# A fused state-space and expert layer on one Trainium2 core: low part of the activations by TensorE and ScalarE, stacked router logits, shorter routing, rstd by exp and ln with a Newton step, new due times

## The chip, the core and the metric

The kernel runs on one core of a Trainium2 chip. The core has TensorE (PE; its weight loads are listed apart as PEld), VectorE (DVE), ScalarE (ACT), GpSimd (POOL) and SyncE (SP), which here only issues DMAs. Each engine works through its own queue in order; they meet through semaphores. The metric is the device time of one execution in microseconds, the median of several runs. The profile is one further execution, taken with the hardware profiler.

## The reference

The input `u` has 8 batches of 1024 rows with 256 channels. A small vector `c` per batch gives six modulation vectors. Then, per batch:

```python
h = layernorm(x) * (1 + ca) + sa
x = x + ga * ssm(h)        # selective scan, 16 states per channel
h = layernorm(x) * (1 + cb) + sb
x = x + gb * moe(h)        # 8 experts of 256x256, the best 2 of each row
```

The scan part projects `h` to a step width `dt` (softplus) and to 16 rows each of B and C, runs `h_n[t] = exp(dt*A_n) * h_n[t-1] + dt*u*B_n[t]` over the rows for each of the 16 states n, and sums `h_n * C_n` over n. The expert part takes `softmax(h @ Wg)`, picks the two largest values of each row, divides them by their sum, and adds the two experts' outputs with these gates. Because the choice of experts depends on small differences, the matrix products there are made from a high and a low part of each operand (`hi`, `lo`; `wg_hi`, `wg_lo`; `we_hi`, `we_lo`), each rounded to the matmul's faster type, with the product of the two low parts left out.

## The kernel before, in words

The 8 x 1024 rows are cut into 16 stages of 512 rows (`CL`), two per batch. A stage has three parts, and stages overlap: while one is in its scans, the one before is in its experts and the one after in its front.

- `front(s)`: statistics of the rows (`statistics`, L777 and L780 on DVE), the factors (`factors`), normalised rows (`normalize`, L822, ACT), transposes to channels (`to_channels`, L852, PE), modulation out of PSUM (`modulate`, L863, ACT), projections (L915, L946), softplus (L952).
- `state(s, n)` for n = 0 to 15: a broadcast load of a row of B and of C (`bc`, SP), `v = du * B` (L1012, POOL), two decays `a = exp(dt * A)` (L1023, ACT), two scans (L1034, DVE), and the product with C: on DVE (`hcD`, L1044) for 10 of 16 states on average, on POOL (`hs`, L1049) for the others. PE adds these products up in PSUM with transposing matmuls (L1097).
- `back(s)`: residual add (L1133, DVE), statistics and factors of the second layernorm, normalising, transposes, the high and low part, router logits, routing, expert products (`expert_pair`, L1310, PE), weighting by the gates (L1388, ACT), summing (L1398, PE), and a storing DMA that adds (L1463, issued by POOL). The last stage's back is cut in two halves and ends on DVE (L1333).

The factors of a layernorm are made per stage for 8 values at once (4 groups of 128 rows of the second layernorm, and 4 of the first one two stages later). ACT copies variance plus eps (L800) and the negated mean (L802) into a small tile `ln`; POOL raises to the power -1/2 (L810) and multiplies with the negated mean (L814). ACT's normalising waits for that.

The high and low part: for each of the two channel halves j, the transposed rows lie in a PSUM tile `pt`. ACT writes the modulated value to SBUF as `hi`, rounded (L863), writes the modulated value again in place into `pt` (L863), and DVE writes `lo = pt - hi` (L1169). The logits are six matmuls into 8 PSUM rows (L1195): `hi` with `wg_hi`, `hi` with `wg_lo`, `lo` with `wg_hi`, for two halves each. ACT copies them out (L1202), PE transposes them back (L1206), and 16 small DVE instructions, with an exponential on ACT as the third step, make the gates (L1225 to L1240, then L1244).

The buffers are rings: four of `v`, three PSUM banks of `a`, two of `y`, one of `ma`, and two of `psm`, which serve transposes, projections, logits and expert products alike.

The order of instructions on every engine is written by a planner (`Plan.emit`). Each step has a kind, an engine, an assumed cost and a due time: the time of its stage plus an entry of the table `DUE`, one per kind and, where it has five, per phase (first stage, second, middle, last but one, last). The planner simulates the engines with these costs and always takes the ready step that is due first; `PATIENCE` says how long an engine may be kept idle for a more urgent step. The order so found is fixed by dependencies; what it costs on the chip is another matter.

Of the kernel before, what the change touches and what calls it, by code (L numbers as in the profile page):

```python
# [10 lines left out]
F32 = mybir.dt.float32  # L11
# [6 lines left out]
P = 128  # L18
CL = 512
# [11 lines left out]
AHEAD = 1010.84  # L31
PATIENCE = {"ACT": 0.15, "DVE": 0.31, "PE": 0.32, "POOL": 0.26, "SP": 0}
# [5 lines left out]
    "-1/2": -610.4,  # L38
    "load c": -1959.77,
    "load wmod0": -1959.2,  # L40
    "load wmod1": -1903.73,
    "load wmod2": -1904.33,
    "load wmod3": -1902,
    "load W_x": -1905.67,
    "load W_dt": -1902.95,
    "load b_dt": -1896.67,
    "load A": -1896.69,
    "load D": -1905.33,
    "load Wg": 23.65,
    "Wg hi": 25.6,  # L50
    "Wg lo": -1879.07,
    "c^T": 19.14,
    "exp c": 576.64,
    "1 + exp c": -171.26,
    "1 / c": -583.34,
    "silu c": 49.75,
    "mod1": 597.1,
    "mod1 out": 214.25,
    "mod1 + 1": -23.47,
    "mod2": -1859.82,  # L60
    "mod2 out": -158.07,
    "mod3": 229.79,
    "mod3 out": -128.45,
    "mod3 + 1": -812.43,
    "ga0": -205.9,
    "ga1": -118.55,
    "ga2": -138.57,
    "ga3": -194.1,
    "gb0": 46.87,
    "gb1": 211.85,  # L70
    "gb2": -132.77,
    "gb3": -2055.94,
    "ga mod": -1469.96,
    "ga mod D": 75.2,
    "1 / ga": -434.12,
    "gb^T": -1935.95,
    "gb out": -1918.95,
    "gb store": -2004.44,
    "W_x^T": 597.29,
    "W_x out": -3.67,  # L80
    "W_dt^T": -1851.32,
    "W_dt out": -85.73,
    "exp A": -10.89,
    "-A": -388.67,
    "be rows": -3.96,
    "be hi": -24.41,
    "be lo": -124.92,
    "be": 74.87,
    "eps": -5318.24,
    "gates hi": (-1934.68, -2774.13, 20.33, -39.94, 880.55),  # L90
    "gates lo": (-26.36, -2354.31, -688.15, -51.05, -108.76),
    "load be": -1860.49,
    "iw": -610.42,
    "load x": (-1905.45, -1873.57, -1877.87, -1851.67, -345.66),
    "stats1": (224.71, 130.11, 139.36, -25.7, -59.05),
    "aggr1": (213.04, 114.8, -308.72, -24.67, 2.36),
    "before1": (-102.85, 91.85, 2.54, -14.87, -18.75),
    "rstd1": (-1104.41, -1916.02, -121.49, -268.12, -120.91),
    "shift1": (-507.66, -410.48, -1091.47, 527.46, 48.83),
    "norm1": (-144.62, -217.6, 35.93, 471.97, 36.59),  # L100
    "trans1_0": (-1936.2, -1160.43, -2075.71, -328.08, -365),
    "modg_0": (-1701.88, 396.46, -461.17, -6.71, -105.52),
    "modD_0": (-1695.18, -131.34, -462.04, -397.38, -105.23),
    "trans1_1": (-388.21, -18.09, -54.78, -626.82, -11.83),
    "modg_1": (-50.33, -1935.21, -197.83, -9.86, -10.79),
    "modD_1": (-11.21, -1916.99, -81.27, -9.63, -23.55),
    "W_x / ga": (66.75, 401.9, 25.85, -49.61, 434.89),
    "proj": (-596.85, -706.64, -714.41, -84.24, -74.21),
    "rows": (-2173.39, -2045.69, -3586.53, -10.82, -2052.7),
    "spill": (-4069.73, -5330.21, -46.16, -311.17, 432.09),  # L110
    "dt0": (-45.16, -658.43, -1891.19, -1934.24, -76.75),
    "softplus0": (-1126.61, -39.94, -137.57, -2844.14, -16.53),
    "dt1": (-2318.21, -2801.94, -207.93, -1934.26, -398.3),
    "softplus1": (-1126.2, -132.53, -379.84, -2844.16, -28.04),
    "du": (-195.14, -2811.82, -615.21, -365.67, -2224.29),
    "load B, C": (-5316.63, -1003.95, -1855.19, -4111.06, -3714.47),
    "v": (-12.17, -164.66, 175.11, 576.96, 952.78),
    "a0": (-22.27, -4.61, -6.54, -5.76, -3.99),
    "a1": (-22.41, -4.9, -6.15, -6.69, -4.35),
    "scan0": (-141.18, -335.17, -38.46, -51.65, -37.62),  # L120
    "keep0": (-1141.13, -1001.73, -2670.6, -1274.64, -1043.43),
    "C0": (-158.99, -48.75, -78.37, -397.8, -49.3),
    "scan1": (254.21, -7.15, -37.67, -52.31, -38.52),
    "keep1": (-281.8, -71.4, -191.93, -1247.6, -175.93),
    "C1": (-927.57, -102.36, -383.08, -272.81, -85.21),
    "C": (-434.46, -982.76, -611.91, -346.76, -4070.99),
    "y D": (-45.12, -33.67, -1893.89, -3.99, 105.31),
    "y": (-692.43, -142.1, -4.58, -4.37, -52.76),
    "y C": (-691.09, -2044.02, -79.98, -1517.96, -52.81),
    "load We": -1855,  # L130
    "We hi": -9.52,
    "We lo": -13.87,
    "x + y": (-1479.33, -1886.74, -1168.73, -231.3, 149.03),
    "store x": (-922.68, -81.4, -352.75, -1815.49, -3867.78),
    "stats2": (-1494.52, -143.82, -1171.26, -54.3, -45.3),
    "aggr2": (-211.14, -109.77, -383.59, -45.32, -9.65),
    "before2": (-6.93, 939.25, -95.98, -81.58, 4.88),
    "rstd2": (-1311.51, -927.35, -919.37, -30.48, -1009.27),
    "shift2": (-289.83, -684.01, -16.58, -27.32, -1671.91),
    "norm2": (-1.27, -217.09, 3.69, -457.58, 32.8),  # L140
    "trans2_0": (-119.41, -234.62, -25.53, -50.95, -76.58),
    "hi0": (-141.55, -203.81, -1226.77, -71.08, -264.52),
    "mod2_0": (-2325.4, 23.63, -1516.83, 17.71, 8.96),
    "lo0": (-954.37, -2006.41, -590.6, 934.22, -43.41),
    "trans2_1": (-68.72, -46.84, -1.98, -2278.83, -10.41),
    "hi1": (1.23, -85.95, -1275.97, -1245.79, 101.74),
    "mod2_1": (-321.5, -1489.76, -82.34, 2.7, -325.68),
    "lo1": (-1141.17, -296.15, -3856.65, 5.32, -1526.54),
    "logits^T": (-724.23, -896.69, -969.16, -194.29, -2895.23),
    "logits out": (-1885.54, -25.88, 4.38, -1907.25, -252.75),  # L150
    "logits": (-1228.11, -85.65, -1913.27, -106.24, -61.81),
    "route": (-1101.97, -1134.93, -1307.99, -656.85, -170.03),
    "gates": (-23.84, -155.06, -1508.55, -606.87, -165.13),
    "gates^T": (407.78, -236.26, -474.82, -43.28, -53.64),
    "gates out": (-77.16, -201.21, -201.01, -1117.77, 23.17),
    "biases": (-1847.78, -40.94, -21.25, 21.25, 22.67),
    "expert0": (-47.23, -150.46, 2.39, -24.85, 59.33),
    "weigh0": (-1667.95, -187.39, -1697.15, 581.79, -169.94),
    "sum0": (154.3, 300.84, -65.34, 25.8, 428.26),
    "gb": (-58.36, -0.34, -1235.11, 1080.88, -11.47),  # L160
    "turn": (45.89, -1931.1, -368.57, -9.4, 45.02),
    "out": (15.32, -128.7, -182.23, -5.57, 44.86),
# [4 lines left out]
    "load gb": (-157.01, -157.01, -157.01, -157.01, -165.58),  # L167
    "last bias": -13.22,
    "last": 89.02,
    "last expert": -11.99,  # L170
    "last store": -219.81,
}

# [1351 lines left out]
```

## Time and profile before

| | us |
|---|---|
| median of 3 runs | 1079.51 |
| lowest, highest | 1077.4, 1081.53 |
| the profiled execution, its own time | 1078.12 |
| its span, first to last instruction | 1076.2 |

| engine | busy us | share of the span | instructions |
|---|---|---|---|
| DVE | 976.5 | 91% | 1506 |
| PE | 948.7 | 88% | 5525 |
| POOL | 928.3 | 86% | 454 |
| ACT | 840.0 | 78% | 1835 |

The mean granted TensorE clock is 0.948 of full speed. Busy time counts each engine by itself; PE's is modelled in part, because matmuls are pipelined. A line such as "L1169 DVE TENSOR_TENSOR lo<-pt,hi" names the line of the kernel, the engine, the operation, and the tile that is written from the tiles that are read. Idle time of an engine is listed with what ended it; an engine that isn't the bottleneck may be idle at no cost.

### The profile page before, as it was taken

What the parts mean: (1) busy time and instruction counts of PE and PEld (TensorE: products, weight loads), DVE (VectorE), ACT (ScalarE), POOL (GpSimd) and SP (SyncE); (2) the same over time, 40 slices, a digit from 0 to 9 for tenths busy, and PEclk for the clock granted to TensorE, in tenths of its full rate; (3) what the DMA queues carried; (4) which work ended last, traced back from release to release, by engine and by line L of the source; (5) the groups of instructions that cost most, each with busy time, mean ns of one, the idle gap of its engine ahead of it and who ended that gap; (6) DMA issues with size and microseconds to landing.
All of it is one profiled execution on the core that took longest, in us unless ns stands there. A gap on an engine that the chain in (4) does not pass through costs nothing. (4 is left out here: it accounts for less than half of the span.)

```text
span 1076.2 us, 16579 instructions
## 1 busy us (share of the span) xinstructions
PE 948.7 (88%) x5525; PEld 746.9 (69%) x5525; DVE 976.5 (91%) x1506; ACT 840.0 (78%) x1835; POOL 928.3 (86%) x454
## 2 busy tenths in 40 slices
PE   6556897997989989898999999898998989899997
PEld 3444675775777858686776868677786767777765
DVE  4699897989999999999999999999999998989957
ACT  5755577887799877988799887988898788887651
POOL 3899776899999999899999999999999989888700
PEclk9666798998999989999999999999899999999999
DMA  6445333447545555454554653554555554365202
GB/s 208 143 176 176 137 139 112 144 165 192 173 162 160 176 159 177 131 185 157 153 202 120 208 164 138 169 179 157 151 195 143 175 155 159 119 178 153 102 1 44
DMA packets 67956, 165.13 MB, mean 153 GB/s; under 512 B 7056, under 2 KB 34080, under 8 KB 67872
## 3 DMA queue, kind: packets, MB, share of 16 engines
q1 hardware_dynamic: 59952, 156.23, 43.1%
q0 software_dynamic: 7920, 7.87, 5.3%
q8 instruction: 43, 0.70, 0.3%
q14 instruction: 41, 0.34, 0.1%
HBM read 146.76 MB, written 17.31 MB: 152 GB/s over the span
## 5 line engine op out<-in xcount | busy, mean ns | idle before, releaser
L1012 POOL TENSOR_TENSOR v<-du,bc 128x1024 f32<-128x1024 f32 x255 | 610.2, 2423 | 54.5 <-DMA bc<-bcd 35.7
L1023 ACT ACTIVATE a<-dt,negA 128x512 f32<-128x512 f32 x512 | 347.1, 692 | 54.8 <-DVE hcD L1044 45.0
L1049 POOL TENSOR_TENSOR hs<-hs,bc 128x1024 f32<-128x1024 f32 x96 | 232.3, 2419 | 16.2 <-ACT carry L1040 5.0
L1044 DVE TENSOR_TENSOR hcD<-a,bc 128x512 f32<-128x512 f32 x320 | 213.6, 682 | 15.1 <-ACT carry L1040 7.4
L1388 ACT ACTIVATE wt<-pe,G 128x256 f32<-128x256 f32 x480 | 200.8, 468 | 33.8 <-PE pe L1310 26.5
L1034 DVE TENSOR_TENSOR_SCAN a<-a,v 128x512 f32<-128x512 f32 x166 | 195.7, 1212 | 23.5 <-ACT a L1023 17.7
L1097 PE MATMUL y<-ident,hcD 128*128 128x128 f32 x1280 | 185.8, 286 | 30.9 <-DVE hcD L1044 30.7
L1034 DVE TENSOR_TENSOR_SCAN a<-a,carry,v 128x512 f32<-128x512 f32 x154 | 196.3, 1278 | 9.8 <-ACT a L1023 7.0
L1097 PEld LDWEIGHTS y<-ident,hcD 128*128 128x128 f32 x1280 | 154.8, 148 | 49.0 <-DVE hcD L1044 37.8
L1310 PE MATMUL pe<-we_hi,hi 128*128 128x512 f32 x512 | 181.7, 436 | 3.4 <-DVE lo L1169 1.1
L1310 PE MATMUL pe<-we_hi,lo 128*128 128x512 f32 x512 | 162.6, 399 | 0.0
L1310 PE MATMUL pe<-we_lo,hi 128*128 128x512 f32 x512 | 162.1, 398 | 0.0
L1398 PE MATMUL ma<-ident,wt 128*128 128x128 f32 x960 | 139.7, 274 | 0.6 <-ACT wt L1388 0.4
L1097 PE MATMUL y<-ident,hs 128*128 128x128 f32 x768 | 111.0, 290 | 24.0 <-POOL hs L1049 23.4
L1097 PEld LDWEIGHTS y<-ident,hs 128*128 128x128 f32 x768 | 92.0, 148 | 50.9 <-POOL hs L1049 40.5
L1398 PEld LDWEIGHTS ma<-ident,wt 128*128 128x128 f32 x960 | 112.5, 140 | 21.4 <-issue 4.6
L1034 DVE TENSOR_TENSOR_SCAN hs<-a,carry,v 128x512 f32<-128x512 f32 x102 | 126.0, 1268 | 1.3 <-ACT a L1023 1.3
L1310 PEld LDWEIGHTS pe<-we_lo,hi 128*128 128x128 f32 x512 | 97.1, 190 | 23.7
L1310 PEld LDWEIGHTS pe<-we_hi,lo 128*128 128x128 f32 x512 | 96.9, 189 | 23.7
L1034 DVE TENSOR_TENSOR_SCAN hs<-a,v 128x512 f32<-128x512 f32 x90 | 106.4, 1206 | 4.3 <-ACT a L1023 4.2
L1310 PEld LDWEIGHTS pe<-we_hi,hi 128*128 128x128 f32 x512 | 82.0, 192 | 16.6 <-ACT wt L1388 4.1
L822 ACT ACTIVATE xn<-x,ln 128x256 f32<-128x256 f32 x128 | 72.9, 598 | 1.6 <-POOL ln L814 1.6
(126 smaller groups left out, 969.2 us busy)
## 6 DMA issues: line engine op xcount, KB each, us to landing
bc<-bcd SPq DMA_DIRECT2D x256, 512.0 KB, 4.0
x<-in_L_attn_u_dram SPq DMA_DIRECT2D x16, 512.0 KB, 4.0
out_dram<-x SPq DMA_DIRECT2D x15, 512.0 KB, 3.0
out_dram<-of POOLq DMA_DIRECT2D x15, 512.0 KB, 9.1
wf<-in_L_ffn_We_dram SPq DMA_DIRECT2D x8, 256.0 KB, 4.0
wm<-in_L_wmod_dram SPq DMA_DIRECT2D x2, 512.0 KB
bcd<-xd SPq DMA_DIRECT2D x32, 32.0 KB, 3.7
wm<-in_L_wmod_dram SPq DMA_DIRECT2D x2, 256.0 KB, 6.0
```

The source lines that it names most:

```text
L822: nc.scalar.activation(new("xn", xn, [P, TG, D])[:, k, :], T[x][:, k0 + k, :], AF.Identity, bias=T[ln][:, 1, o + k : o + k + 1], scale=T[l ...
L1012: nc.gpsimd.tensor_tensor(new("v", v, [P, DC, CL])[:, :, :cl], T["du", s][:, :, :cl], both(T[bc][:, 0, :cl]), ALU.mult,)
L1023: nc.scalar.activation(new("a", a + (j,), [P, CL])[:, :cl], T["dt", s][:, j, :cl], AF.Exp, scale=negA[:, j, n : n + 1],)
L1034: nc.vector.tensor_tensor_scan(part(j), T[a + (j,)][:, :cl], T[v][:, j, :cl], init, ALU.mult, ALU.add)
L1044: nc.vector.tensor_tensor(new("hcD", hc, [P, DC, CL])[:, j, :cl], part(j), T[bc][:, 1, :cl], ALU.mult)
L1049: nc.gpsimd.tensor_tensor(o, o, both(T[bc][:, 1, :cl]), ALU.mult)
L1097: nc.tensor.matmul(new("y", y, [P, 2, D])[:, k % 2, j * P : (j + 1) * P], T[src][:, j, k * P : (k + 1) * P], ident, is_transpose=True, sta ...
L1310: nc.tensor.matmul(pe, T[v][:, j, k * P : (k + 1) * P], w[:, j, 2 * q : 2 * q + 2, :].rearrange("p e d -> p (e d)"), start=n == 0, stop=n ...
L1388: nc.scalar.activation(new("wt", wt, [P, 2, D])[:, i, :], T["pe", s, part, q, k][:, i * D : (i + 1) * D], AF.Copy, scale=T[G][:, k, e : e ...
L1398: nc.tensor.matmul(o[:, j, (k % 2) * P : (k % 2 + 1) * P], T["wt", s, q, k][:, i, j * P : (j + 1) * P], ident, is_transpose=True, start=Fa ...
```

## The change

It has five parts.

1. The low part. ACT now first modulates `pt` in place, then copies it, rounded, to `hi`. PE adds minus `hi` into the same PSUM tile by a matmul with a negative identity `negI` (step "less"), and ACT copies the rest out as `lo`. DVE has no part in it.
2. The logits. High and low part of `Wg` stand side by side in one tile of 16 columns. Two products of `hi` with all 16 and two of `lo` with the first 8 replace the six. The transposes back become matmuls with a 16 x 8 matrix `fold` of two identities, which add the two halves.
3. The routing. The sum of the two gates' numerators is 1 plus the second one, as the largest is exp(0). ACT makes it right after the second maximum is known; a reduction on DVE goes.
4. The factors. ACT makes a first guess of rstd as exp(-0.5 ln(variance + eps)), then the two copies as before, in one step of four instructions; POOL makes one Newton step and the shift, in five. Both are steps of the planner that carry the table "exp"; when it returns from softplus, the emitted program names the table that holds exponential and logarithm.
5. The order. All due times, `AHEAD` and `PATIENCE` are new, the costs of the changed steps too, and a few dependencies are added for the planner: expert products of a stage come after its logits have been copied out and after the last expert product of the stage before, and the turning back of finished sums keeps its order.

The diff without the due times:

```diff
-AHEAD = 1010.84
-PATIENCE = {"ACT": 0.15, "DVE": 0.31, "PE": 0.32, "POOL": 0.26, "SP": 0}
+AHEAD = 1438.35
+PATIENCE = {"ACT": 0.15, "DVE": 0.42, "PE": 0.33, "POOL": 0.56, "SP": 0.24}
...
+        table = "exp"
         for i in order:
+            if ops[i]["table"] not in (None, table):
+                table = ops[i]["table"]
+                if table == "exp":
+                    tc.nc.scalar.preload_act_table_set("natural_log_exp_and_others")
             ops[i]["fn"]()
...
-        add("-1/2", "DVE", 0.01, lambda: nc.vector.memset(mhalf, -0.5), w=[("mhalf",)])
+        add("-I", "ACT", 0.25, lambda: nc.scalar.activation(negI, ident, AF.Copy, scale=-1.0), w=[("negI",)])
...
+        wgf = [wg_2[:, :, i * E : (i + 1) * E] for i in range(2)]
+        add("fold", "DVE", 0.07, lambda: nc.vector.reduce_sum(fold, ident[: 2 * E, : 2 * E].rearrange("p (i e) -> p e i", i=2), AX.X), w=[("wg", 2)])
...
-                nc.scalar.activation(row(2), T[st][:, :n, 7], AF.Identity, bias=eps)
-                nc.scalar.activation(row(3), T[st][:, :n, 6], AF.Copy, scale=-1.0)
-            "rstd" + n_, "POOL", 0.88 + 0.035 * n, t, lambda: nc.gpsimd.tensor_tensor(row(0), row(2), mhalf[:, :n], ALU.pow),
-            "shift" + n_, "POOL", 0.16, t, lambda: nc.gpsimd.tensor_tensor(row(1), row(3), row(0), ALU.mult),
+        def guess():
+            nc.scalar.activation(row(2), T[st][:, :n, 7], AF.Ln, bias=eps)
+            nc.scalar.activation(row(0), row(2), AF.Exp, scale=-0.5)
+            nc.scalar.activation(row(2), T[st][:, :n, 7], AF.Identity, bias=eps)
+            nc.scalar.activation(row(3), T[st][:, :n, 6], AF.Copy, scale=-1.0)
+        def newton():
+            r, m, v, tt = row(0), row(1), row(2), nc.gpsimd.tensor_tensor
+            tt(m, r, r, ALU.mult)
+            tt(m, m, v, ALU.mult)
+            nc.gpsimd.tensor_scalar(m, m, -0.5, 1.5, ALU.mult, ALU.add)
+            tt(r, r, m, ALU.mult)
+            tt(m, row(3), r, ALU.mult)
+            "before" + n_, "ACT", 0.75, t, guess, r=[st, ("eps",)], w=[ln], ring=("ln", ln), table="exp",
+        plan.add("rstd" + n_, "POOL", 0.85, t, newton, r=[st], w=[ln])
...
         def mod_hi(j):
-            modulate(new("hi", hi, [P, DC, CL], F32R)[:, j], 2, s, j, modT[:, 3:], part)
+            nc.scalar.copy(new("hi", hi, [P, DC, CL], F32R)[:, j, :cl], T["pt", 2, s, part, j][:, :cl])
+        def less(j):
+            nc.tensor.matmul(
+                T["pt", 2, s, part, j][:, :cl], negI, T[hi][:, j, :cl], start=False, stop=True,
         def low(j):
-            nc.vector.tensor_tensor(
-                new("lo", lo, [P, DC, CL], F32R)[:, j, :cl], T["pt", 2, s, part, j][:, :cl],
-                T[hi][:, j, :cl].bitcast(F32), ALU.subtract,
+            nc.scalar.copy(new("lo", lo, [P, DC, CL], F32R)[:, j, :cl], T["pt", 2, s, part, j][:, :cl])
...
-            for v, w in products:
+            for v, m in ((hi, 2 * E), (lo, E)):
                 for j in range(DC):
-                        lg[:E, :cl], (wg_hi, wg_lo)[w][:, j, :], T[v][:, j, :cl],
+                        lg[:m, :cl], wg_2[:, j, :m], T[v][:, j, :cl], start=n == 0, stop=n == 2 * DC - 1,
...
-                nc.tensor.transpose(
-                    T[pl][:, k * E : (k + 1) * E], T[lgt][:, k * P : (k + 1) * P], ident[:E, :E]
+                nc.tensor.matmul(
+                    T[pl][:, k * E : (k + 1) * E], T[lgt][:, k * P : (k + 1) * P], fold, start=True, stop=True
...
-            lambda: red(col(3), view(1), AX.X, ALU.add),
+            nc.scalar.activation(col(3), col(1), AF.Identity, bias=1.0)
...
+            turns = [("lgd", s)] + ([("ex", s - 1)] if s else [])
+            turned_ = [("td", s - 1 + p, 1 - p)] if s + p else []
+            if 2 * s + p > 2:
+                turns.append(("td", s - 2 + p, 1 - p))
-                        r=[hi, lo] + wes, w=[pe], ring=("psm", pe), duty=0.88, cold=1.76,
+                        r=[hi, lo] + wes + turns,
+                        w=[pe] + ([("ex", s)] if m == ends else []), ring=("psm", pe), duty=0.88, cold=1.76,
```

## The prediction

> **What bounds the kernel now.** I read the page first, for the share of each engine:
>
> ```profile
> PE 948.7 (88%) x5525; PEld 746.9 (69%) x5525; DVE 976.5 (91%) x1506; ACT 840.0 (78%) x1835; POOL 928.3 (86%) x454
> ```
>
> Four engines are nearly full, and these means include a start and a tail. So I asked for the windows (busy us and instruction count of PE, PEld, DVE, ACT, POOL, then clock, DMA share, GB/s); the last row is the undisturbed middle:
>
> ```profile
> 120.00:180.00 60.00, 53.77 (x295) 41.98 (x293) 49.71 (x70) 45.05 (x95) 42.35 (x21) 0.87 0.37 132
> 480.00:540.00 60.00, 54.57 (x334) 43.10 (x333) 58.67 (x85) 50.87 (x101) 57.59 (x28) 1.00 0.55 167
> 840.00:900.00 60.00, 54.85 (x342) 43.75 (x343) 55.51 (x83) 50.09 (x97) 56.97 (x28) 1.00 0.55 168
> 300.00:900.00 600.00, 554.08 (x3370) 439.37 (x3369) 571.74 (x851) 513.93 (x1121) 572.13 (x269) 0.99 0.53 165
> ```
>
> DVE and POOL are tied at 95%, PE follows at 92%, ACT at 86%. A stage is as long as the distance of its residual adds (L1133): they start from 94.5 to 1031.0 us, fifteen stages apart, so 62.4 us. Per stage DVE then has 59.5 us of work, POOL 59.5, PE 57.6, ACT 53.4. Next, what POOL waits for in the same 600 us (total us, times, longest):
>
> ```profile
> POOL v L1012 <- DMA bc<-bcd: 9.9, 10, 1.8
> POOL hs L1049 <- DVE hs L1034: 2.9, 4, 1.4
> POOL v L1012 <- DVE pl L1233: 2.8, 1, 2.8
> POOL v L1012 <- DVE pl L1237: 1.8, 1, 1.8
> POOL v L1012 <- DVE rt L1225: 1.8, 1, 1.8
> ```
>
> POOL's v does not read the routing tiles. It needs one of four v buffers, which a scan on DVE frees, and the routing run stands before that scan. With two rows of 0.4 and 0.3, POOL waits 10.0 us for DVE: 1.04 us a stage. DVE waits for POOL only 2.9 us. Thus DVE leads by a little and POOL has no room behind it.
>
> **The change part by part.** The durations come from these groups (busy us, mean ns, idle before):
>
> ```profile
> L863 ACT ACTIVATE hi<-pt,modT 128x512 fp32r<-128x512 f32 (+1 forms) x34 | 25.5, 756 | 2.3 <-PE pt L852 2.3
> L1169 DVE TENSOR_TENSOR lo<-pt,hi 128x512 fp32r<-128x512 f32 (+1 forms) x34 | 22.1, 649 | 7.1 <-ACT pt L863 6.9
> L1419 ACT COPY of<-pf 128x512 f32<-128x512 f32 x30 | 17.5, 584 | 6.1 <-PE pf L1413 6.0
> L1195 PE MATMUL pl<-hi,wg_lo 128*8 128x512 f32 (+1 forms) x34 | 10.4, 389 | 0.0
> L1239 DVE TENSOR_REDUCE rt<-pl 128x4 f32<-128x32 f32 (+1 forms) x17 | 3.2, 189 | 0.6
> L800 ACT ACTIVATE ln<-st,eps 128x8 f32<-128x8 f32 (+2 forms) x19 | 5.8, 305 | 24.4 <-DVE st L780 24.4
> L802 ACT ACTIVATE ln<-st 128x8 f32<-128x8 f32 (+2 forms) x19 | 3.8, 202 | 0.0
> ```
>
> and, because a mean hides the overlap of neighbours, from the distance of starts in the timelines (start, duration) of DVE and POOL, and for the table switch of ACT:
>
> ```profile
> 429.51 0.69 DVE L1169 TENSOR_TENSOR lo<-pt,hi 128x512 fp32r<-128x512 f32 x1 [0.33 <-ACT pt L863]
> 430.12 1.22 DVE L1034 TENSOR_TENSOR_SCAN hs<-a,v 128x512 f32<-128x512 f32 x1
> ```
> ```profile
> 421.78 1.66 POOL L810 TENSOR_TENSOR ln<-ln,mhalf 128x8 f32<-128x8 f32 x1
> 423.51 0.20 POOL L814 TENSOR_TENSOR ln<-ln 128x8 f32<-128x8 f32 x1
> 423.67 9.44 POOL L1012 TENSOR_TENSOR v<-du,bc 128x1024 f32<-128x1024 f32 x4
> ```
> ```profile
> 395.50 1.28 ACT L952 ACT_TABLE_LOAD   x1
> 396.79 1.26 ACT L952 ACTIVATE dt<-pv,bdt 128x512 f32<-128x512 f32 x2
> 398.07 1.28 ACT L1023 ACT_TABLE_LOAD   x1
> ```
>
> DVE. A subtraction `lo` takes 0.61 us of the queue (429.51 to 430.12); two go per stage, 1.22. One reduction of the routing goes; its neighbours start about 0.22 apart. Together −1.44 us: 59.5 becomes 58.1. The reciprocal newly waits for ACT (`both_e`), which is issued after the eighth routing step, six DVE steps (1.3 us) earlier: hidden. If one 0.69 us exponential stands ahead of it on ACT it is still hidden; two cost up to 0.3, and gates and scans are queued behind.
>
> POOL. Power and shift occupy 421.78 to 423.67, 1.89 us. Newton is five small instructions, each on the result of the one before. L814 is the nearest row: 0.20 long, 0.16 to the next start, 0.07 after the power it depends on. So 5 × 0.27 = 1.35, with 5 × 0.16 = 0.80 as the low end and 1.89 (no gain) as the high end, since the fused multiply-add is not shown. I take 1.35, as the steps depend on each other: −0.54 us a stage, 59.0 left (0 to −1.1). Before Newton POOL waits for four instructions on ACT instead of two, about 0.5 us longer; v and C are queued behind it and the scans wait for v, but up to three finished v's cover that. Without this cover it would take the gain.
>
> ACT. `hi` turns from a modulation into a plain PSUM copy, 0.756 to 0.584; `lo` is a second such copy. Two of each a stage: 2 × (0.584 − 0.17) = +0.82. Ln costs as L800 (0.305), exp as L802 (0.20), `both_e` about 0.2. Sum +1.5 us: 53.4 becomes 54.9, the emptiest engine still. The Trainium skill's page "ScalarE: Activation LUTs" (Rules for kernel authors) speaks against this move: it gives adds and multiplies to VectorE, up to about three times faster per element in bf16. By that ratio `lo` would take 1.9 us on ACT, an estimate from that page, and ACT would hold 57.6 us a stage. The rows above have fp32 out of PSUM, 0.649 on DVE against 0.584 on ACT, so the measurement decides for the move.
>
> Tables. Ln needs the table of logarithm and exponential, which the program loads at the start and, now explicitly, after each pair of softplus. The rows show a switch as 1.28 us plus 0.02, with no drain behind it; there are 33 loads now, and I expect 33. A statistics step that fell between two softplus would add two, 2.6 us on ACT; it has 9 us a stage to hide that, so nothing to the sum, +2.6 as the other bound. The same page (What ACT_TABLE_LOAD costs) counts 2.66 us for one switch with its drain, and lists one set that holds both functions; by it such an accident would cost 5.3 us.
>
> PE. Logits drop from six products to four; 10.4 us over 34 is 0.31 each, −0.62 a stage. Two `less` products of the same 512 columns give +0.62. The four `fold` products against four small transposes: 0 to +0.4. Net 0. But `less` waits on ACT for `hi`, and all of PE's queue stands behind it. The nearest row is the logits' own trip: L1206 sat idle 10.5 us for ACT's copy in 17 stages' parts, 0.62 a trip. Two trips are +1.24 us of waiting, and PE has 4.8 us free per stage: hidden, while no third of PE's slack is wanted elsewhere.
>
> Setup. `fold` and `-I` replace a memset; 0.2 us of DVE and ACT in a start where DVE is busy 3.75 us of the first ten: nothing. The two longer chains do show at the ends: about +0.5 us before the first norm (ACT 0.5 longer, POOL 1.35 against 1.03 + 0.20), and about +1.0 in the tail, where factors and low part of the last rows precede the last experts.
>
> **The sum.** DVE's relief alone is not the gain: POOL at 59.0 is now the fullest. POOL loses 0.54 us of work and, DVE being ahead, I take half of its 1.04 us of waiting for DVE: −1.06 a stage. Fifteen stages give −15.9, the ends +1.5: −14.4. The profiled execution took 1078.12 (span 1076.2 and 1.9 around it), the median of the runs is 1079.51, 1.4 above. 1063.7 for the first is **1065** for the median. Ends: with no wait returned −8.1 + 1.5, so 1073; with POOL keeping up, DVE sets −1.44/0.953 = −1.51 a stage, −22.7 + 1.5, so 1058.
>
> The due times are all new, and they move every queue, the loads of B and C on SP included. Their order cannot be read off the diff. Its price, from the rows: DVE's idle time differs between 1.3 and 4.5 us in undisturbed windows of 60, and 120 to 180 us has 7.5 us less DVE work than the middle. So ±1 us a stage for part of the run, some ±8 us.
>
> **Rivals.**
> 1. *DVE sets the pace throughout and the order also closes early holes.* −21.2 and up to −8 more: 1050 to 1058. For it: POOL hardly keeps DVE waiting now. Against: POOL would run at 97%, while loads of B and C alone hold it up for 1.6%.
> 2. *Given back.* Newton as long as the power, or an order with 1 us more idle time a stage: −14.4 + 8 to −14.4 + 15.9, so 1073 to 1081, about no change. For it: POOL's step is the one unmeasured price.
> 3. *Slower: the trip through PE.* The two shared PSUM buffers carry transposes, logits and expert products. One is held from the transpose at 427.17 to the end of `lo` at 430.2; the added trip lengthens that, and `less` blocks the queue. An uncovered chain, 427.80 to 430.2, is 2.4 us. With PE at 97% at best, the stage is (57.6 + 2 × trip)/0.97; it passes 62.4 from 1.5 us a trip on. At 1.8 it is 63.1: +10.5 and +1.5, so 1091; at 2.4, 1109. Against: 0.62 in the nearest row, and PE has sums and y transposes to fill with.
> 4. *It does not do what it says:* loads of tables double. 33 more at 1.3 us is 2.7 a stage on ACT, within its slack; the time stays near the forecast.
>
> **How the numbers follow.** A change under 0.5% (1074 to 1085) cannot be told from none. Forecast, with 4 in it, 0.56; rival 1 0.15; rival 2 0.11; rival 3 0.18. Rival 2 sends 0.01 to each side. Faster 0.72, same 0.09, slower 0.19. The range runs from 1049, below rival 1, to 1087, which leaves out most of rival 3 (0.15) and some 0.04 below.
>
> **What would show it.** Right: no DVE `lo`, 34 ACT copies near 0.58; five POOL steps under 0.3 each; 33 table loads; residual adds 61.3 apart; from 300 to 900 us DVE clearly under POOL, and POOL's waits for DVE near 5 us. Rival 3 would show as PE idle before `less` above 1.5 us each. Wrong would be POOL steps near 0.38, or residual adds 62.4 or more apart.

## The result, and the profile after

The changed kernel takes 1087.41 us (median of 4 runs, 1086.31 to 1089.02); the kernel before, on the same chip, 1078.76 (1077.4 to 1081.53). The ratio is 1.0064, with a 95% interval of 1.0043 to 1.0084: a little slower, where 1065 was forecast. The profiled execution took 1087.69 us with a span of 1085.9 and a mean granted clock of 0.951 (before 1078.12, 1076.2 and 0.948).

The busy shares, from the page of the changed kernel:

```profile
PE 955.0 (88%) x5589; PEld 757.0 (70%) x5589; DVE 952.0 (88%) x1455; ACT 865.2 (80%) x1925; POOL 914.2 (84%) x511
```

The work went where the change says: DVE has 24.5 us less, POOL 14.1 less, ACT 25.2 more, PE 6.3 more. In the window from 300 to 900 us (columns as before) the middle shows it too, but no engine is above 93% of it any more, where DVE and POOL were at 95%:

```profile
300.00:900.00 600.00, 555.66 (x3395) 443.61 (x3393) 548.80 (x812) 525.01 (x1159) 555.70 (x295) 0.99 0.53 162
```

DVE fell from 571.74 to 548.80 and POOL from 572.13 to 555.70, and yet a stage is no shorter, as the residual adds below show. What POOL and DVE wait for in this stretch (total us, times, longest) shows where the freed time went:

```profile
POOL v L1025 <- DMA bc<-bcd: 18.7, 14, 2.4
POOL hs L1062 <- DVE hs L1047: 18.5, 12, 1.6
```
```profile
DVE a L1047 <- POOL v L1025: 14.1, 11, 1.7
DVE hs L1047 <- ACT a L1036: 10.4, 8, 1.6
```

Before, these four were 9.9, 2.9, 2.9 and 2.2 us. POOL's products with C (`hs`) now wait for DVE's scans, DVE's scans wait for POOL's `v`, and `v` waits longer for its loads. The two engines take turns in waiting for each other.

The groups of the new steps (busy us, mean ns, idle before) and POOL's Newton step in the timeline:

```profile
L1188 ACT CAST lo<-pt 128x512 fp32r<-128x512 f32 (+1 forms) x34 | 19.2, 566 | 6.7 <-PE pt L1182 6.7
L1176 ACT CAST hi<-pt 128x512 fp32r<-128x512 f32 (+1 forms) x34 | 19.0, 562 | 0.7
L1224 PE MATMUL pl<-fold,lg 16*128 16x8 f32 x128 | 17.0, 254 | 0.2 <-ACT lg L1220 0.2
L1182 PE MATMUL pt<-hi,negI 128*128 128x512 f32 (+1 forms) x34 | 16.6, 489 | 1.6 <-ACT hi L1176 1.5
```
```profile
419.91 0.21 POOL L819 TENSOR_TENSOR ln<-ln 128x8 f32<-128x8 f32 x1
...
421.05 0.20 POOL L823 TENSOR_TENSOR ln<-ln 128x8 f32<-128x8 f32 x1
421.21 2.40 POOL L1025 TENSOR_TENSOR v<-du,bc 128x1024 f32<-128x1024 f32 x1
```

POOL needs 1.30 us (419.91 to 421.21) in place of 1.89. Each `less` has little idle time ahead of it, and ACT waits only 6.7 us in all for it.

The time itself is read from the residual adds (engine, count, shortest, median and longest ns, first and last start; x and y are the tiles), for before and for after:

```profile
L1133 DVE TENSOR_TENSOR x<-x,y x32: 653/671/687, 94.5 to 1031.0; 128x512 f32<-128x512 f32 x32
```
```profile
L1146 DVE TENSOR_TENSOR x<-x,y x32: 659/671/689, 92.4 to 1030.5; 128x512 f32<-128x512 f32 x32
```

The way from the first add to the last, divided by fifteen, is called a stage here: 62.43 us before, 62.54 after. From the last add to the end of the span are 45.2 us before and 55.4 after. So the 9.7 us of the span are -2.1 at the start, +1.6 over fifteen stages and +10.2 behind the last add. The +1.6 is not spread evenly: the eleventh residual add, five stages in, starts at 412.9 us where it started at 418.1, and the changed kernel gives this lead back in the ten stages behind it. The windows of these tails, before and after:

```profile
1031.00:1076.20 45.20, 36.89 (x171) 26.29 (x169) 27.41 (x82) 14.04 (x40) 3.57 (x7) 0.96 0.13 27
```
```profile
1030.50:1085.90 55.40, 41.49 (x202) 30.63 (x200) 25.79 (x80) 18.07 (x54) 3.65 (x13) 0.94 0.11 22
```

PE has 4.6 us more work left at the last add: expert products of the last but one stage that the new due times put off. It is idle 5.6 us more: 13.91 of 55.4 against 8.31 of 45.2. The last stage's back runs in two halves, and half of that idle time is one wait for the gates of the second half, where PE did not wait before; in PE's timeline:

```profile
1060.61 0.39 PE L1299 MATMUL pl<-ident,gs 128*24 128x128 f32 x2 [2.72 <-POOL gs L1293]
```

The other half lies behind PE's last matmul. It ends 5.7 us before the span does in the kernel before, and 8.6 in the changed one (at 1077.29), where the last weighted adds (to 1080.62) and a storing DMA that POOL issues at 1078.21 still follow; before, that DMA was issued at 1050.91.

### The profile page after: what moved, and what is told of

Same layout as the page of the kernel before. It is cut to its first block, busy times and chain, and to the rows that moved or that the text cites. A ratio compares the mean times of both kernels' runs of the same rounds, so it can differ in the third digit from the quotient of the medians.

```text
span 1085.9 us, 16828 instructions
## 1 busy us (share of the span) xinstructions
PE 955.0 (88%) x5589; PEld 757.0 (70%) x5589; DVE 952.0 (88%) x1455; ACT 865.2 (80%) x1925; POOL 914.2 (84%) x511
## 5 line engine op out<-in xcount | busy, mean ns | idle before, releaser
L1025 POOL TENSOR_TENSOR v<-du,bc 128x1024 f32<-128x1024 f32 x255 | 616.7, 2488 | 44.4 <-DMA bc<-bcd 39.3
L1062 POOL TENSOR_TENSOR hs<-hs,bc 128x1024 f32<-128x1024 f32 x96 | 240.1, 2501 | 32.6 <-DVE hs L1047 24.7
L1411 ACT ACTIVATE wt<-pe,G 128x256 f32<-128x256 f32 x480 | 204.8, 470 | 21.4 <-PE pe L1333 20.7
L1110 PE MATMUL y<-ident,hcD 128*128 128x128 f32 x1280 | 182.7, 286 | 16.9 <-DVE hcD L1057 16.7
L1333 PE MATMUL pe<-we_hi,hi 128*128 128x512 f32 x512 | 186.1, 445 | 5.5 <-ACT dt L965 2.5
L1421 PE MATMUL ma<-ident,wt 128*128 128x128 f32 x960 | 142.6, 276 | 0.4 <-ACT wt L1411 0.2
L1110 PE MATMUL y<-ident,hs 128*128 128x128 f32 x768 | 108.0, 285 | 26.6 <-POOL hs L1062 26.5
L834 ACT ACTIVATE xn<-x,ln 128x256 f32<-128x256 f32 x128 | 70.2, 595 | 11.4 <-POOL ln L823 11.2
```

What stands on the lines that cost most here:

```text
L834: nc.scalar.activation(new("xn", xn, [P, TG, D])[:, k, :], T[x][:, k0 + k, :], AF.Identity, bias=T[ln][:, 1, o + k : o + k + 1], scale=T[l ...
L1025: nc.gpsimd.tensor_tensor(new("v", v, [P, DC, CL])[:, :, :cl], T["du", s][:, :, :cl], both(T[bc][:, 0, :cl]), ALU.mult,)
L1062: nc.gpsimd.tensor_tensor(o, o, both(T[bc][:, 1, :cl]), ALU.mult)
L1110: nc.tensor.matmul(new("y", y, [P, 2, D])[:, k % 2, j * P : (j + 1) * P], T[src][:, j, k * P : (k + 1) * P], ident, is_transpose=True, sta ...
L1333: nc.tensor.matmul(pe, T[v][:, j, k * P : (k + 1) * P], w[:, j, 2 * q : 2 * q + 2, :].rearrange("p e d -> p (e d)"), start=n == 0, stop=n ...
L1411: nc.scalar.activation(new("wt", wt, [P, 2, D])[:, i, :], T["pe", s, part, q, k][:, i * D : (i + 1) * D], AF.Copy, scale=T[G][:, k, e : e ...
```

## The experiments

"Old order" means the due times, `AHEAD` and `PATIENCE` of the kernel before. The table has the medians, the ratio to the kernel before that ran beside it on the same chip, and from each one's profiled execution the same three numbers as above. These three come from one execution each (that of e1 was the fastest of its four, 4.7 us under their median), so small differences between them mean little.

| kernel | median us | ratio (95%) | us a stage | behind the last add | span |
|---|---|---|---|---|---|
| before | 1078.76 | | 62.43 | 45.2 | 1076.2 |
| after | 1087.41 | 1.0064 (1.0043 to 1.0084) | 62.54 | 55.4 | 1085.9 |
| e1 | 1095.52 | 1.0146 (1.0113 to 1.0178) | 63.06 | 48.5 | 1089.1 |
| e2 | 1095.34 | 1.0136 (1.0111 to 1.0162) | 63.35 | 47.8 | 1093.8 |
| e3 | 1079.41 | 0.9998 (0.9977 to 1.0019) | 62.27 | 45.7 | 1074.6 |
| e4 | 1076.33 | 0.9965 (0.995 to 0.998) | 62.23 | 45.4 | 1073.6 |
| e5 | 1076.66 | 0.9956 (0.9925 to 0.9988) | 62.14 | 44.7 | 1071.7 |
| e6 | 1096.95 | 1.0136 (1.0121 to 1.0151) | 63.45 | 47.4 | 1094.5 |
| e7 | 1080.68 | 0.9988 (0.9972 to 1.0004) | 62.50 | 45.3 | 1078.9 |
| e8 | 1076.75 | 0.9949 (0.9928 to 0.997) | 62.31 | 44.1 | 1074.1 |
| e9 | 1067.78 | 0.9874 (0.9844 to 0.9903) | 61.60 | 44.7 | 1063.9 |
| e10 | 1090.74 | 1.0083 (1.0057 to 1.011) | 62.56 | 58.1 | 1089.0 |
| e11 | 1077.24 | 0.9965 (0.9949 to 0.998) | 62.19 | 46.0 | 1075.6 |
| e12 | 1086.36 | 1.0043 (1.0024 to 1.0062) | 62.45 | 56.1 | 1086.1 |
| e13 | 1089.57 | 1.0103 (1.0082 to 1.0124) | 63.23 | 46.8 | 1089.9 |
| e14 | 1087.76 | 1.0087 (1.0062 to 1.0112) | 62.81 | 47.5 | 1085.6 |
| e15 | 1099.69 | 1.0185 (1.0157 to 1.0213) | 63.42 | 54.6 | 1098.7 |
| e16 | 1079.54 | 0.9991 (0.9978 to 1.0003) | 62.47 | 45.9 | 1078.4 |

**Operations or order (e1 to e4).** The first question was whether the new operations or the new order lose the time. e1 puts all four changes of operations at the old order's places:

> Every changed operation of the four parts (low part, stacked logits, shorter routing, Newton) put into the kernel before at the places that its old order gives to the steps they replace; due times, planner costs and so the order of all steps are those of before. Theory A (the operations save what was priced, the new order lost it): the stage goes from 62.4 to about 61.4 us and the time to 1064 to 1071. Theory B (VectorE and GpSimd were not what paced the middle, so relief there is worth nothing; TensorE and ScalarE get 0.4 and 1.6 us more a stage): 1077 to 1085, stage 62.4 or longer. Theory C (the trip through TensorE stalls its queue): 1090 or more, with idle time before the products with negI.

At 1095.52 us the time is where Theory C has it: the operations themselves lose in the old order, and the new order is better for them by 0.8%. Theory C's other sign is missing: PE is idle for 6.5 us before all 34 products with -I together. Three more kernels put one part each there.

e2, the low part:

```diff
-            modulate(new("hi", hi, [P, DC, CL], F32R)[:, j], 2, s, j, modT[:, 3:], part)
+            modulate(T["pt", 2, s, part, j], 2, s, j, modT[:, 3:], part)
...
+            nc.scalar.copy(new("hi", hi, [P, DC, CL], F32R)[:, j, :cl], T["pt", 2, s, part, j][:, :cl])
...
-            nc.vector.tensor_tensor(
...
-                T[hi][:, j, :cl].bitcast(F32), ALU.subtract,
...
+            nc.tensor.matmul(
+                T["pt", 2, s, part, j][:, :cl], negI, T[hi][:, j, :cl], start=False, stop=True,
...
+            nc.scalar.copy(new("lo", lo, [P, DC, CL], F32R)[:, j, :cl], T["pt", 2, s, part, j][:, :cl])
```

> Only the low part by TensorE and ScalarE, in the order of before. Theory A: VectorE loses 1.2 us a stage, time 1068 to 1074. Theory B: 1077 to 1084. Theory C: 1088 or more, most of what the run with all four parts loses.

e3, the Newton step, with its two new activations in the step that makes variance plus eps:

```diff
-            lambda: nc.gpsimd.tensor_tensor(row(0), row(2), mhalf[:, :n], ALU.pow),
+            newton,
```

> Only exp and ln with a Newton step in place of the power, in the order of before. Theory A: GpSimd loses 0.6 us a stage, ScalarE gains 0.5: 1070 to 1076. Theory B: no change, 1076 to 1081. All theories: 33 table loads.

e4, the stacked logits and the shorter routing:

```diff
-            for v, w in products:
+            for v, m in ((hi, 2 * E), (lo, E)):
...
-            lambda: red(col(3), view(1), AX.X, ALU.add),
+            lambda: None,
```

> Only the stacked logits and the shorter routing, in the order of before. VectorE loses 0.2 us a stage; TensorE loses two products of 0.3 us and gets four more passes of the fold of 0.13 us. Theory A: 1074 to 1078. Theory B: 1077 to 1081. A loss above 4 us would say that the fold delays the routing.

The low part alone loses as much as all parts together: 63.35 us a stage, 0.92 more than before. Newton moves the time by nothing that can be measured, although POOL is 95% busy. Logits and routing together gain 0.35%; which of the two does was not tried.

**What of the low part costs (e5 to e8).** It takes a subtraction from DVE, gives ACT two copies, and sends the value through PE. e5 takes the subtraction away alone:

```diff
-                f"lo{j}", "DVE", cost("DVE", 0.6, cl), t, lambda j=j: low(j), r=[pt, hi + (j,)],
+                f"lo{j}", "DVE", cost("DVE", 0.6, cl), t, lambda: None, r=[pt, hi + (j,)],
...
-            for v, w in ((hi, we_hi), (hi, we_lo), (lo, we_hi)):
+            for v, w in ((hi, we_hi), (hi, we_lo), (hi, we_hi)):
```

> The kernel before, in its order, without the two subtractions of the low part on VectorE and with nothing in their place (the products read hi where they read lo, so the low part of the activations is left out). VectorE has 1.2 us less a stage, no other engine more. Theory A (VectorE paces the middle): stage 61.2 to 61.6, 1062 to 1070. Theory B (it does not): stage 62.2 or more, 1076 to 1081.

DVE loses 1.2 us of work a stage and the stage only 0.29. The window from 300 to 900 us shows POOL as full as before (572.13) and DVE no longer so:

```profile
300.00:900.00 600.00, 555.79 (x3367) 441.49 (x3366) 561.43 (x830) 512.08 (x1119) 571.90 (x269) 0.98 0.54 165
```

e6 is e2 with the copy of `lo` made by DVE (against e2):

```diff
-            nc.scalar.copy(new("lo", lo, [P, DC, CL], F32R)[:, j, :cl], T["pt", 2, s, part, j][:, :cl])
+            nc.vector.tensor_copy(new("lo", lo, [P, DC, CL], F32R)[:, j, :cl], T["pt", 2, s, part, j][:, :cl])
```

> As the run with the low part alone in the old order, but VectorE copies the rest out of PSUM instead of ScalarE: the trip through TensorE stays, ScalarE gets no copy more, VectorE no relief. Theory C (the trip costs): 1088 to 1096, as with ScalarE. Theory D (ScalarE's two added copies cost, because its queue is full just there, and the decays behind them come late to the scans): 1079 to 1085.

It loses as much as e2, with a busier DVE and a less busy ACT, so ACT's copies are not what costs and Theory D is out. The timeline of e6 shows one such trip:

```profile
431.38 0.71 PE L1313 MATMUL pe<-we_hi,hi 128*128 128x512 f32 x2
431.92 0.63 PE L1313 MATMUL pe<-we_lo,hi 128*128 128x512 f32 x2
432.39 0.63 PE L1313 MATMUL pe<-we_hi,lo 128*128 128x512 f32 x2
432.86 0.40 PE L1171 MATMUL pt<-hi,negI 128*128 128x512 f32 x1
...
433.29 0.69 DVE L1175 CAST lo<-pt 128x512 fp32r<-128x512 f32 x1 [1.10 <-PE pt L1171]
```

PE is not idle at all. The product with -I stands in its queue behind an expert pair of 1.5 us, and DVE, in order too, stands still for 1.10 us until it has run. Over the kernel DVE waits 26.6 us at this place.

e7 is e2 without the trip, ACT's copies kept (against e2):

```diff
-            nc.tensor.matmul(
-                T["pt", 2, s, part, j][:, :cl], negI, T[hi][:, j, :cl], start=False, stop=True,
-                skip_group_check=True,
-            )
```

> As the run with the low part alone in the old order, but without the products with negI on TensorE: ScalarE copies the modulated value itself into lo (so lo holds the whole value and the low part is wrong). ScalarE's copies and VectorE's relief stay, the trip is gone. Theory C: 1066 to 1080. Theory D: 1088 to 1096, VectorE waiting some 15 us for decays from 300 to 900 us as with the trip.

With ACT's copies and no trip the kernel is no slower than before (0.9988; 0.7 us above Theory C's range, 7 under Theory D's). The trip is what costs. DVE has its relief here as well, and e5, with the relief and no copies, gained 0.3% more, though the intervals overlap; so the copies take about that back, if anything.

e8 asks what PE is worth: the expert pairs of two of the eight experts leave out the product with `lo`.

```diff
-            for v, w in ((hi, we_hi), (hi, we_lo), (lo, we_hi)):
+            for v, w in ((hi, we_hi), (hi, we_lo), (lo, we_hi)) if q else ((hi, we_hi), (hi, we_lo)):
```

> The kernel before, in its order, with the product of lo left out in one of four groups of expert products (the low part's share there is left out): TensorE has 8 passes of 0.23 us less a stage, 1.9 us. If TensorE paces the middle: stage 60.6 to 61.4, 1050 to 1064. If it does not: 1075 to 1081, with a gain of some us at the end alone.

Less PE work brings 0.5%, for 16.0 us less of listed PE time (932.7 in place of 948.7): PE's own load has a price of about a third of itself.

**Who sets the pace (e9).** e5's edit and, on POOL, a multiplication in place of the power, which takes 1.4 us a stage off it:

```diff
-            lambda: nc.gpsimd.tensor_tensor(row(0), row(2), mhalf[:, :n], ALU.pow),
+            lambda: nc.gpsimd.tensor_tensor(row(0), row(2), mhalf[:, :n], ALU.mult),
```

> The kernel before, in its order, with both reliefs at once: without the two subtractions of the low part (as in the run without them; the low part of the activations is left out), and with a product in place of the power on GpSimd (so rstd is not computed). VectorE has 1.2 us less a stage, GpSimd 1.4 less. Theory E (VectorE and GpSimd pace the middle together, so that either relief alone is lost to the other): stage 61.0 to 61.6, 1060 to 1069, clearly more than the two alone (4.7 and 0 us) give together. Theory F (the middle is held by trips between all engines, and a relief of any one gives a quarter of itself): 1070 to 1076.

The two reliefs together gain 1.26%, against 0.44% for DVE's alone (e5). The window has all three engines within 3.3 us of each other:

```profile
300.00:900.00 600.00, 563.29 (x3406) 447.11 (x3405) 566.50 (x840) 516.48 (x1131) 564.75 (x272) 0.98 0.54 167
```

DVE and POOL did pace the kernel together, as Theory E and the prediction read it, and PE is then as busy as they are. POOL's relief of 1.4 us by itself was not run; its smaller one, Newton in e3, gained nothing.

**The new order (e10 to e12).** e10 keeps it and takes the trip out: DVE subtracts again, no product with -I.

```diff
-            nc.tensor.matmul(
-                T["pt", 2, s, part, j][:, :cl], negI, T[hi][:, j, :cl], start=False, stop=True,
...
-            nc.scalar.copy(new("lo", lo, [P, DC, CL], F32R)[:, j, :cl], T["pt", 2, s, part, j][:, :cl])
+            nc.vector.tensor_tensor(
+                new("lo", lo, [P, DC, CL], F32R)[:, j, :cl], T["pt", 2, s, part, j][:, :cl],
+                T[hi][:, j, :cl].bitcast(F32), ALU.subtract,
```

> The changed kernel in its new order, but the low part is a subtraction on VectorE at the place of ScalarE's copy, and the products with negI are left away. Theory G (the new order covers the trip, which is why its middle is shorter than in the old order with the same operations): 1086 to 1093, since VectorE gets 1.2 us a stage back. Theory H (the trip still costs there, about half of what it costs in the old order): 1077 to 1083.

Undoing the low part gains nothing there (Theory G), and the tail is no shorter: 58.1 us. DVE gets its subtraction back with this edit, so the trip by itself was not priced in the new order; ACT's copies without the trip were not run there. e11 joins the edits of e3 and e4, which makes the fourth corner: the old order with everything but the low part:

> Newton, stacked logits and shorter routing in the order of before, the low part left with VectorE. The two alone gave 0 and -4 us: 1073 to 1077, and faster than both kernels. If the two reliefs help each other: 1070 to 1073.

With e1, e10 and the changed kernel it makes a square of ratios: old order 0.9965 without the trip and 1.0146 with it; new order 1.0083 and 1.0064. "Trip" stands for the whole low part here. Each alone costs over 1%, and they do not add: in the new order the low part costs nothing, but the order brings its own loss of 1.2%. e11 equals e4, and both beat the two kernels of the case. e11 and e10 also settle where the mutual waits of POOL and DVE come from. Their operations differ little, in how ACT makes `hi` and in how the factors' steps are grouped; this is POOL's wait for DVE's scans from 300 to 900 us, e11 and then e10:

```profile
POOL hs L1071 <- DVE hs L1056: 2.7, 4, 1.3
```
```profile
POOL hs L1062 <- DVE hs L1047: 14.5, 13, 1.9
```

DVE's wait for POOL's `v` goes from 2.3 to 12.3 us with it. These waits belong to the new order, not to the new operations.

e12 changes one due time of the new order, so that the next to last turn of sums and its store come early:

```diff
-    "turn": (287.17, 1.8, 2.77, 272.21, 322.97),
+    "turn": (287.17, 1.8, 2.77, -9.4, 322.97),
```

> The changed kernel with one due time changed: the turning back of the sums in the last stage but one is due 281 us earlier (-9.4 as before, instead of 272.21). In the profile after, its last store leaves 7 us after the last expert product and ends last. If the late store is what is paid: 1082 to 1085. If the end is set by the last expert products and VectorE behind them: 1086 to 1088.

That store is now issued at 1052.02, but the time hardly moves: PE's last expert product ends at 1079.57 in place of 1076.79. The late store is no more than a small part of the tail.

**Where `less` stands (e13, e14).** The same as e2 and e1, but the product with -I is emitted directly behind the copy of `hi`, ahead of the expert products:

```diff
         def mod(j):
             nc.scalar.copy(new("hi", hi, [P, DC, CL], F32R)[:, j, :cl], T["pt", 2, s, part, j][:, :cl])
+            nc.tensor.matmul(
+                T["pt", 2, s, part, j][:, :cl], negI, T[hi][:, j, :cl], start=False, stop=True,
...
         def low(j):
-            nc.tensor.matmul(
-                T["pt", 2, s, part, j][:, :cl], negI, T[hi][:, j, :cl], start=False, stop=True,
```

> The low part alone in the order before, as e2, but PE's product with -I is emitted directly behind ScalarE's copy of hi instead of at the place of lo. Theory Q (the trip costs because the product stands behind expert products that were queued before it, and the copier waits): most of the 14.6 us of e2 comes back, 1077 to 1086 us, and ScalarE's wait for PE before lo falls from 13.7 us to under 6. Theory S (a trip costs the same wherever it stands, since now PE has to stand still for ScalarE's copy): 1091 to 1100 us, with PE idle before this product at 20 us or more (15.1 in e2).

> All four parts in the order before, as e1, with the product with -I directly behind the copy of hi. Theory Q: e13's result less the 3.7 us that stacked logits and routing gave in e4, 1073 to 1083 us; if it is under 1076 it is the best version of the whole change. Theory S: 1090 us or more, as e1 (1095.5).

Neither theory holds as stated. ACT's wait before `lo` fell from 13.7 to 3.7 us, as Theory Q has it, but the time came back only by a quarter (1.0136 to 1.0103, intervals that overlap) and in e14 by two fifths (1.0146 to 1.0087). ACT's wait and PE's wait at the trip over the whole kernel, e2 and then e13:

```profile
ACT lo L1175 <- PE pt L1171: 13.7, 22, 2.1
PE pt L1171 <- ACT hi L1168: 6.1, 4, 3.6
```
```profile
ACT lo L1175 <- PE pt L1169: 3.7, 8, 0.9
PE pt L1169 <- ACT hi L1168: 11.6, 15, 3.9
```

Two queues that run in order meet twice in a trip, and moving the meeting point moves part of the wait from ACT to PE. It is not the whole account: ACT waits 10.0 us less and PE 5.5 us more, DVE's waits for `a` are back to 9.5 us (9.3 without the trip, in e7), and yet most of the loss is there. Where the rest of e13's loss sits is not shown. One rival can be settled from the traces, that the shared PSUM buffer is held longer: from the start of the modulation to the end of `lo` it took 2.71 us in e7, 3.19 in e2 and 2.85 in e13 (means of the twenty from 300 to 900 us), so e13 holds it nearly as briefly as e7 and is still 0.73 us a stage slower.

**The tail again (e15).** The new order with the expert steps of the last but one stage due as in the middle stages:

```diff
-    "expert0": (-1919.87, -0.43, -0.06, 27.6, 62.09),
+    "expert0": (-1919.87, -0.43, -0.06, -0.06, 62.09),
...
-    "expert1": (-66.23, -2684.46, -0.61, 62.46, 98.21),
+    "expert1": (-66.23, -2684.46, -0.61, -0.61, 98.21),
```

These are two of the seven lines.

> The changed kernel with seven due times of the last but one stage (its expert products, their weighting, sums and biases) set to those of the middle stages, so that this stage's experts are not put off past the last residual adds. Theory I (the put-off products are a loss of their own): the last residual add stays near 1030 us, the end behind it falls from 55.4 to 45 to 48 us, time 1077 to 1081 us. Theory H (the same work only stands elsewhere; in the last third PE and the engines around it are what ends the kernel): the end falls to about 45 us, but the last residual add comes 5 to 15 us later, and the time stays at 1084 to 1096 us.

Theory H is right about the last add, which comes 13.6 us later, but wrong about the end, and the time is above both ranges. The end stays at 54.6 us, although the put-off products are gone (132 PE records in place of 202). PE's longest wait and two windows of this tail show what took their place:

```profile
PE pt L864 <- ACT xn L834: 5.0, 1, 5.0
```
```profile
1039.00:1049.00 10.00, 2.97 (x23) 2.19 (x21) 6.61 (x15) 2.92 (x11) 2.79 (x9) 0.73 0.40 52
1049.00:1059.00 10.00, 8.14 (x25) 5.82 (x26) 2.56 (x15) 5.68 (x16) 0.39 (x2) 0.50 0.00 1
```

PE is nearly empty for ten microseconds while the last scans, adds and statistics run, and in the next ten it gets half its clock. In the changed kernel the put-off products stand at this place, so putting them off was no plain waste.

**PE's time or the waiting (e16).** One more product, low with low, in two expert pairs of each stage, as many as the products with -I:

```diff
+            more = int(q == 0 and k < 2)
...
+            if more:
+                nc.tensor.matmul(
+                    pe, T[lo][:, 0, k * P : (k + 1) * P],
+                    we_lo[:, 0, 2 * q : 2 * q + 2, :].rearrange("p e d -> p (e d)"), start=False, stop=True,
+                )
```

> The kernel before, with one more product of 128x512 in two of the expert pairs of each stage (low with low, 34 in all, as many as the products with -I), behind the six that are there: the same work for PE as the trip, but nobody waits anew. Theory W (the trip's price is PE's own time): 34 times 0.40 to 0.45 us is 13.6 to 15.3 us of PE, and most of it shows, 1087 us or more. Theory T (the price is the waiting in a round trip between two queues in order): e8 took 1.9 us a stage off PE for a gain of 5.5 us, so 0.8 us a stage more should cost some 2.4 us, 1078 to 1083 us.

The time stays (0.9991), as Theory T has it. But the load is not quite the same. PE's busy time in the profile rises from 948.7 us only to 952.2 in e16, where the new product follows its neighbours without a gap, but from 948.6 (e7) to 962.1 in e2. At the price of e8, 5.5 us of time for 16.0 of PE, these 13.5 us would cost 4.6, an estimate from these rows, and the trip costs about 16 (e2 against e7). So most of the trip's price is not PE's work. That leaves the waiting between the queues, of which e2 and e6 show a part and e13 shows that the part is not all.

## Why the prediction was wrong

The sum had -15.9 us for fifteen stages and +1.5 for the ends. Measured were +1.6 and +8.1. The error of the forecast for the profiled execution, 1087.7 against 1063.7, is thus 17.5 us in the middle and 6.6 at the ends. The time also lies 0.4 us above the range, and the kernel is slower where a gain was forecast.

Two steps failed. The sum counted a gain of 1.06 us a stage, where the same reliefs were worth far less and the trip was taken as hidden; and it counted the new order as nothing, with "some ±8 us" around it. The runs put prices in their place, in a chain from the kernel before to the changed one (stages from one execution each). Newton, logits and routing in the old order gave -0.24 us a stage (e11). The new order gained 4.2 us at the start, but took 0.37 a stage and 12.1 us behind the last add (e10 against e11); by the ratios it costs 1.2%, some 12.8 us, more than the ±8. The new low part in this order gave -0.02 a stage, which is nothing (the changed kernel against e10).

*Right, step by step.* DVE's work falls as priced, by 24.5 us. Newton was priced at 1.35 us and is 1.30. ACT's additions were 1.5 us a stage; 25.2 over some 16 stages is 1.6, and e7 shows little price for them. There are 33 table loads, 16 of them on the line that names the table, each 1.283 us. e9 confirms that DVE and POOL are tied. PE's net of 0 was low, since `less` took 0.49 us and not 0.31 and `fold` 0.6 us a stage more than the small transposes and not 0 to 0.4; PE has 6.3 us more in all, which at e8's price is 2 us.

*Wrong in the middle, first: what the relief is worth.* "The sum" turned -1.44 us on DVE and -0.54 on POOL into -1.06 a stage. Without any trip, in the old order, -0.22 and -0.54 gave -0.24 (e11); -1.2 and nothing gave -0.29 (e5); -1.2 and -1.4 gave -0.83 (e9). The forecast's pair lies between the last two, nearer to e5, so the term was about twice too large, as an estimate from these rows. Half of POOL's wait for DVE was taken as given back, with a sign near 5 us for 300 to 900 us; in the changed kernel this wait is 18.5 us there, from 10.0, and e10 against e11 shows that the new order brings it.

*Wrong in the middle, second: the trip counted as hidden.* "Two trips are +1.24 us of waiting, and PE has 4.8 us free per stage: hidden." The row behind 0.62 us a trip was misread: its 10.5 us add PE's 4.1 and the weight loads' 6.4 before the same instructions. That the low part then costs 0.92 us a stage in the old order (e2) is near 1.24 by luck. The cover was wrong there. The step asked whether PE can afford to wait, but PE seldom waited (in e2 6.1 us in four places). The waiting fell on the engine behind the trip: DVE in e6, and in e2 ACT, whose decays for the scans were queued behind `lo`, so that DVE's waits for `a` in the 600 us were longer than before (6.3) and than with the copies alone (9.3 in e7):

```profile
DVE a L1036 <- ACT a L1025: 14.7, 18, 1.8
```

By e13 this is a part of the price and not all of it. Rival 3 had the trip by name, but with PE as the engine that pays. Its sign, PE idle above 1.5 us before each `less`, came in no run, and that its stage of 63.1 us is what e1 shows (63.06) is chance: it was worked out with PE at 97%, and PE is at 92% in e1 (553.24 of 600 us). In the changed kernel ACT waits 6.7 us before `lo` in place of 13.7, and by e10 the low part costs nothing there; but it brings no gain either.

*Wrong at the end: the order.* It had +1.0 in the tail and "some ±8 us" for the new due times, and the tail alone took 10.2. e1 has all operations and 3.3 us more tail, e10 has no trip and 12.9 more, so most of it belongs to the order. (Part of e10's 12.9 is a stretch of 10.2 us at half PE's clock, which the changed kernel does not have.) No single step carries it: neither the late store (e12) nor the put-off products (e15), each of which turned into later work or a hole when it was moved. Why the new order's tail is long is open beyond that. The timeline suggests that its last two residual adds start 0.6 us apart in place of 1.6 and the first transposes follow the last one by 6.5 us in place of 3.8, but no run tried that. Why the new order makes POOL and DVE wait for each other is open too: that it comes from the new places of `hs` and `v` is read from the trace.

The Trainium skill's page "ScalarE: Activation LUTs" (Rules for kernel authors) gives adds to VectorE. The row it was weighed against holds: the copy of `lo` out of PSUM took 0.566 us on ACT and the subtraction 0.649 on DVE, and by e7 against e5 ACT's copies cost some 0.3% at the medians. It was not the change of engine that cost most.

## What to carry to other kernels

Between engines that each run a queue in order, price a new round trip by who stands behind its two meeting points, not by the free time of the engine it passes: in the old order here two products a stage cost nothing when they followed others of their kind, and 1.4% when another engine waited for them in between. Work taken from one of two tied engines gained a quarter of its length here (DVE) or nothing that can be measured (POOL), from both of them a third of the sum. When a change brings a new order, run its operations in the old order and the old operations in the new one before believing either; the part worth having here was the stacked logits with the shorter routing, in the old order.

## What the runs showed of the hardware

Two things were not expected. Products of a 16 x 8 fp32 operand are listed twice (128 records for 64 transposes back, 254 ns each), so `fold` takes 17.0 us of PE where the small transposes took 7.0; that ate most of the 11.2 us that the stacked logits save there (20.9 in place of 32.1), so the gain of e4 is not PE's work (952.0 us in its profile, 3.3 more than before).

And PE's clock fell in tails with gaps. In e15 windows show it at 1.00 up to 1043.6 us, at 0.50 from there to 1060.7 and at 1.00 again behind it; in the 3.4 us before the fall PE was busy for 1.35. In e10 it fell at 1059.3, behind 3.4 us with 1.38 us of PE work, and stayed at 0.50 for 10.2 us. PE waited 2.90 us for the gates around that moment; the changed kernel waits 2.72 us at the same step and keeps 1.00. The Trainium skill's page "TensorE: Matmul & The Clock Gate" (Part 1: The HAM clock gate) gives half rate after an idle window of some 3.4 us. Here the clock fell with less than that: the longest wait of PE in the 3.4 us ahead was 1.78 us in e15, and e15's wait of 5.0 us came behind the fall.
